# Third graph transposed by vector squares behind the degrees' strips, the last graph's product order, and one pair of activations on VectorE

## The chip, the cores and the metric

One NeuronCore of a Trainium2 chip runs the kernel. The metric is the device time of one execution in microseconds (us); the time before is the median of three runs. TensorE (PE) multiplies matrices and transposes through an identity, VectorE (DVE) does elementwise work and statistics, ScalarE (ACT) activations and copies out of PSUM, GpSimd (POOL) elementwise work on SBUF and some DMA issues, and SyncE (SP) only issues DMAs. Each engine executes its own instructions in program order and waits at semaphores; everything is float32.

## The reference

Two graph layers over x of 16 graphs x 1024 nodes x 256 channels with one adjacency of 1024 x 1024.

```python
# layer 0
h = jnp.maximum(_layernorm(x, axis=-1), 0.0)
fea = jnp.transpose(h, (0, 2, 1)); c_adj = jnp.mean(fea, axis=1)
diff = c_adj[:, None, :] - c_adj[:, :, None]
A = jnp.abs(jnp.abs(jax.nn.sigmoid(diff) - 0.5) - 0.5) * 2.0
Wg = adj[None, :, :] * (A + jnp.transpose(A, (0, 2, 1))) * 0.5
q = relu(einsum('bcn,bnm->bcm', fea, Wg) * para)      # split into 4 heads
k, v = split(h @ kv_w)                                 # 4 heads of 64
x = x + softmax(q k^T * scale) v
# layer 1
h = jnp.maximum(_layernorm(x, axis=-1), 0.0)
A_norm = adj + I
deg = A_norm.sum(0) + A_norm.sum(1) - diagonal(A_norm)
agg = (A_norm * rsqrt(deg)[:, None] * rsqrt(deg)[None, :]) @ h
y1 = relu(batchnorm(agg @ W1.T + b1))                  # over all graphs and nodes
x = x + batchnorm(y1 @ W2.T + b2)
```

The batch norms run over all graphs, so their statistics need every graph's products first.

## The kernel before

**Stages.** `attention()` walks over the 16 graphs. Each graph b has 16 steps (4 units of a channel half and a node half, 4 steps each). A step issues the scores of two key tiles (`scores`, L1081), their exps on ScalarE (L1089), the accumulation of the exps on VectorE (L1110, L1113) and the product with the values of the step before (L1124). Between the steps a generator, `background(b)`, supplies the other work in pieces: the keys, values and queries of graph b+1, the second layer's products of graph b-1, norms. What a generator yields is the cost of its piece; 1.71 stands for one piece of eight or so matmuls. A step takes pieces while `done < due`, where `due = total * (step + 1) / 16`; `total` (L1256 to 1259) is thus the pace, and larger than the sum of the costs when the work shall be done ahead of the stage's end. In the last graph `due` is lowered by a further term. A yield of `TOP` puts the next piece at the head of the following step, between scores and values.

**Weaving.** `weave(main, (start, side), ...)` takes one piece of main and then, from piece `start` on, one slot of each side. Sides are ScalarE, VectorE, GpSimd and DMA work and mostly cost 0. When main has ended, what is left of the sides is run through. `soon(action)` queues an action behind the next piece.

**The stage of graph 0.** `background(0)` (L964) first turns graph 1's normed x (`transposed`, 8 TensorE transposes per channel half through PSUM and ScalarE copies, L424 and L430). Then come the keys and values of graph 1 (`keys_values`, 4 + 4 pieces, L174), its queries (`plain_queries`, 16 pieces) and, at the sides: the weights of graph 1 (`weigh`, 17 slots: Abs L508 and Tanh L516 on ScalarE, a product with adj L495 on VectorE in every other slot), the first norm of graph 2 (`Norm(2, True).all()`, 8 slots), the Strassen combinations of the transposed adjacency (`graph`, GpSimd, 8 chunks), and the degrees (`degrees`). Before, four pieces of keys run with two weight slots each; the four pieces of values come at the end, between the two transposed halves of graph 2.

`degrees` loads eight strips of 128 rows of the transposed adjacency (`load_adj_t`, L226), sums each by an in-place ScalarE copy with an accumulator (L241) and takes the diagonal on VectorE (L243, L244). The strips and the adj tiles of the weights (`load_adj`, L192) have one tag in a pool of three buffers, and both loads are issued by SP. A buffer comes free when the last instruction that uses its tile has run.

**Graphs from 3 on** are turned by `squares` instead: VectorE transposes all 32 x 32 squares of a channel half (L438), the result is stored to DRAM (L442), and `gathered` loads it back in four DMAs that put the squares in place (L452).

**The last graph and the end.** `aggregate(15)` multiplies the normed x with seven blocks of the adjacency (Strassen, L174 `pa`), and its additions (L729 to L758) fill at[0] and at[1], the two node halves; the last block completes the lower half of at[0]. `plain_hidden(15)` then makes eight products (`py`): j, the quarter of the hidden units, is the outer loop, g, the node half, the inner. Each is activated (L910), stored (L911) and goes into the statistics (L914), which are aggregated for a j once both g are in (L916). From the fourth product on each is followed by `next(turns[0])`, one turn of `second()`, the second phase: affine parts of the first batch norm (L96, L97, L1386 to L1388), first activations of graph 0 (`relu`, L1453), and after the last product: `relu(1, 0)`, the differences t1s (L1600), `relu(2, 0)`, `relu(3, 0)`, the affine parts of the other half. Then the first products of the phase are issued in this order: m1 of graph 0, m5 of graph 0 (reads t1s), m1 of graph 1, and `graph(0)` with m2, m3, m6, m7, m4; before m4, `combine_4` on GpSimd (L1486) waits until m6 has read its input.

`normed_last()` is woven into the last hidden products of graph 14: it normalises graph 15's halves as soon as the attention has completed them, so that `aggregate(15)` can begin.

Of the kernel before, what the change touches and what calls it, by code (L numbers as in the profile page):

```python
# [12 lines left out]
ALU = mybir.AluOpType  # L13
# [10 lines left out]
def gnn_two_layers_kernel(  # L24
# [12 lines left out]
    nc = tc.nc  # L37
    B, N, C = x.shape
    H1 = w1_t.shape[1]
    NT = N // P  # L40
    CC = C // P
# [3 lines left out]
    NH = N // FB  # L45
# [28 lines left out]
    hsq_d = [dram.tile([P, CC, N], F32, name=f"hsq_d{b}") for b in range(B)]  # L74
# [24 lines left out]
    def layers(shifted):  # L99
# [51 lines left out]
        def weave(main, *sides):  # L151

            for i, cost in enumerate(main):
                for start, side in sides:
                    if i >= start:
                        cost += next(side, 0.0)
                yield cost
            for _, side in sides:
                yield from side

        def double(slots):

            for _ in slots:
                next(slots, None)
                yield 0.0
# [244 lines left out]
        TOP = -1.0  # L410

        def transposed(b, ks, halves=range(NH), meanwhile=None):

            h = hs["a", b]
            for k in ks:
                if 0 in halves:
                    ht = p3.tile([P, N], F32, tag="ht", name=f"ht_{b}_{k}")
                    hts.setdefault(b, []).append(ht)
            for g in halves:
                pts = [bank(f"htp_{b}_{k}_{g}") for k in ks]  # L420
                for j in range(FB // P):
                    t = g * (FB // P) + j
                    for k, pt in zip(ks, pts):
                        nc.tensor.transpose(  # L424
                            pt[:, j * P : (j + 1) * P], h[:, t, k * P : (k + 1) * P], ident
                        )
                    if meanwhile is not None:
                        meanwhile()
                for k, pt in zip(ks, pts):
                    nc.scalar.copy(hts[b][k][:, g * FB : (g + 1) * FB], pt)  # L430

        def squares(b):

            for k in range(CC):
                sq = p1.tile([P, N], F32, tag="sq", name=f"sq_{b}_{k}")
                nc.vector.transpose(  # L438
                    sq.rearrange("p (i t s) -> p i t s", i=NS, s=SQ),
                    hs["a", b][:, :, k * P : (k + 1) * P].rearrange("p t (i s) -> p i t s", s=SQ),  # L440
                )
                nc.gpsimd.dma_start(out=hsq_d[b][:, k], in_=sq)  # L442
                for _ in range(3):
                    yield 0.0

# [448 lines left out]
        def plain_hidden(b):  # L894

            at = ats[b]
            parts = [(g, j) for g in range(NH) for j in range(HC)]
            if b == B - 1:

                parts.sort(key=lambda part: part[1])  # L900
                next(turns[0])
            for n, (g, j) in enumerate(parts):
                i = b * NH + g
                made = bank(f"py_{i}_{j}")
                for k in range(CC):
                    product(
                        made, later["w1"][:, k, j * P : (j + 1) * P], at[g][:, k, :], k == 0, k == CC - 1
                    )
                y = py.tile([P, FB], F32, tag="y", name=f"y_{i}_{j}")
                nc.scalar.activation(y, made, AF.Identity, bias=b1[:, j : j + 1])  # L910
                nc.gpsimd.dma_start(out=y1_d[i][:, j, :], in_=y)  # L911

                def stats(y=y, i=i, j=j):
                    nc.vector.bn_stats(stats1[:, j, i, :], y)  # L914
                    if i == B * NH - 1:
                        nc.vector.bn_aggr(mv1[:, j, :], stats1[:, j].rearrange("p a s -> p (a s)"))  # L916

                soon(stats)
                if b == B - 1 and n >= len(parts) // 2 - 1:
                    soon(lambda: next(turns[0]))  # L920
                yield 1.71
# [42 lines left out]
        def background(b):  # L964

            if b == 0:
                differences(1)
                for k in range(CC):
                    yield TOP
                    transposed(1, (k,))  # L970
                    yield 1.0
                w, products, norm = weighers[1], keys_values(1), Norm(2, True).all()
                yield from weave(islice(products, 4), (0, double(islice(w, 8))))
                asked, build, sums = plain_queries(1), graph(), degrees()
                yield from weave(
                    islice(asked, 13),
                    (0, w),
                    (4, norm),
                    (5, islice(build, 8)),
                    (7, islice(sums, 6)),  # L980
                )
                differences(2)
                yield from weave(asked, (0, build), (0, sums))
                w = weighers[2]
                yield from islice(products, 1)
                yield from weave(islice(products, 2), (0, islice(w, 2)))
                yield TOP
                transposed(2, (0,))
                yield 1.0
                yield from weave(islice(products, 1), (0, islice(w, 1)))  # L990
                yield from islice(w, 1)
                yield TOP
                transposed(2, (1,))
                yield 1.0
                yield from islice(w, AHEAD - 4)
                yield from products
                return
            before = hidden(b - 1)
            gather = aggregate(b - 1)
            if b + 1 < B:  # L1000
                w, products, norm = weighers[b + 1], keys_values(b + 1), normed(b - 1)
                yield from weave(islice(products, 4), (0, islice(w, 4)))
                asked = queries(b + 1)
                yield from weave(islice(asked, 7), (0, double(w)))
                if b == 1:
                    load_later()
                yield from weave(asked, (2, islice(norm, 5)))
                if b + 2 < B:
                    load_x(b + 2, True)
                yield next(gather)  # L1010
                yield from weave(products, (0, norm))
            else:
                yield next(gather)
                yield from weave(endings.pop(), (2, normed(b - 1)))
            if b + 2 < B:
                yield from weave(gather, (0, summed(b + 2)), (1, lately()))
                yield from prepare(b + 2, before)
            elif b + 2 == B:

                yield from weave(gather, (1, lately()))  # L1020
                endings.append(before)
            else:
                yield from weave(gather, (1, lately()))
                yield from weave(before, (0, normed_last()))
# [215 lines left out]
        def attention():  # L1240
# [6 lines left out]
            bg, done, total, top = iter(()), 0.0, 0.0, False  # L1247
            for s in range(len(steps) + 2):
                if s < len(steps):
                    unit, g = steps[s]  # L1250
                    b = unit.at[0]
                    if s % per_graph == 0:
                        run(bg)
                        top = False
                        bg, done = background(b), 0.0
                        total = (37.6 if b > 0 else 41.0) * (b + 1 < B) + 24.0 * (b > 0) + 6.0 * (b == 0)  # L1256
                        total += 12.0 * (0 < b < B - 2) + 25.7 * (b == B - 1) + 3.0 * (b == 0)

                        total -= 10.3 * (b == B - 1)
                    made = scores(*unit.at, g)  # L1260
                    due = total * (s % per_graph + 1) / per_graph
                    if b == B - 1:
                        due -= 0.5 * min(s % per_graph + 1, (per_graph - 1 - s % per_graph) * 0.75)
                else:
                    due += 5.1
# [46 lines left out]
        with st:  # L1312
            if shifted:
                for b in range(B):
# [13 lines left out]
                    norm = Norm(b, False)  # L1328
# [6 lines left out]
            else:  # L1335
# [7 lines left out]
                norm = Norm(0, True)  # L1343
# [26 lines left out]
    def second(kind):  # L1370
# [54 lines left out]
        with st:  # L1425
# [23 lines left out]
            def relu(i, half, js=range(JH)):  # L1449
                scale, sh = aff[half]  # L1450
                for j in js:
                    y = ys[i][:, half * JH + j, :]
                    nc.scalar.activation(  # L1453
                        y, y, AF.Relu, bias=sh[:, j : j + 1], scale=scale[:, j : j + 1]
                    )
# [137 lines left out]
            yield  # L1593
            relu(0, 0, (1,))
            yield
            relu(1, 0)
            second_steps(0)
            b11, b12, _, _ = inputs(0)
            for j in range(JH):
# [128 lines left out]
```

## Time and profile before

| what | us |
|---|---|
| median of three runs | 2458.16 (2457.94 to 2458.37) |
| profiled execution, its own time | 2458.76 |
| its span, first to last instruction | 2457.0 |
| granted TensorE clock, mean | 0.993 |
| stage of graph 0 (first scores to first scores of graph 1) | 54.6 to 160.1 |
| last scores of the attention | 2123.2 |
| aggregate(15) begins | 2144.1 |
| first product of the second phase | 2184.4 |
| last product of the second phase | about 2380 |

Each trace line names a time in us from the start of the span, a duration, the engine, the line of the kernel, and "out<-in" by the program's names; `x` is how many instructions a line merges. What stands in brackets is the idle time of the engine before it and what ended it. The lines of waits give the total, the number and the longest. The lines of one tile or one source line give the minimum, median and maximum duration in ns. Instructions on TensorE are pipelined, so their durations overlap, and the distance between two starts tells what one costs. Completions of DMAs are read from the semaphore events in the trace.

### The profile page before, as it was taken

What the parts mean: (1) busy time and instruction counts of PE and PEld (TensorE: products, weight loads), DVE (VectorE), ACT (ScalarE), POOL (GpSimd) and SP (SyncE); (2) the same over time, 40 slices, a digit from 0 to 9 for tenths busy, and PEclk for the clock granted to TensorE, in tenths of its full rate; (3) what the DMA queues carried; (4) which work ended last, traced back from release to release, by engine and by line L of the source; (5) the groups of instructions that cost most, each with busy time, mean ns of one, the idle gap of its engine ahead of it and who ended that gap; (6) DMA issues with size and microseconds to landing.
All of it is one profiled execution on the core that took longest, in us unless ns stands there. A gap on an engine that the chain in (4) does not pass through costs nothing. (4 is left out here: it accounts for less than half of the span.)

```text
span 2457.0 us, 35930 instructions
## 1 busy us (share of the span) xinstructions
PE 2411.6 (98%) x13290; PEld 831.1 (34%) x13290; DVE 2006.6 (82%) x3104; ACT 1258.2 (51%) x1870; POOL 555.9 (23%) x644
## 2 busy tenths in 40 slices
PE   9999999999999999999999999999999999999994
PEld 4333333333333333333333333333333332334444
DVE  5688888988888888889898888888888878767775
ACT  7774554545464545545454646454454534345554
POOL 1371202111111212020111112121202103136652
PEclk9999999999999999999999999999999999999997
DMA  4675545363545554453636355544535353456559
GB/s 146 199 247 179 171 137 184 114 233 125 204 143 193 171 189 163 148 177 122 214 120 226 122 200 165 195 158 169 172 130 198 116 201 142 144 206 231 194 193 373
DMA packets 204553, 437.18 MB, mean 178 GB/s; under 512 B 21456, under 2 KB 96720, under 8 KB 200272
## 3 DMA queue, kind: packets, MB, share of 16 engines
q1 hardware_dynamic: 173328, 327.29, 39.7%
q0 software_dynamic: 31040, 107.50, 11.7%
q8 instruction: 107, 1.75, 0.3%
q14 instruction: 78, 0.64, 0.1%
HBM read 331.36 MB, written 103.35 MB: 177 GB/s over the span
## 5 line engine op out<-in xcount | busy, mean ns | idle before, releaser
L1089 ACT ACTIVATE p<-sc 128x1024 f32<-128x1024 f32 x512 | 495.4, 1020 | 649.6 <-PE sc L1081 649.6
L1113 DVE TENSOR_TENSOR acc<-acc,p 128x1024 f32<-128x1024 f32 x384 | 471.1, 1227 | 58.7 <-ACT p L1089 37.3
L1081 PE MATMUL sc<-q,k 64*64 64x512 f32 x4096 | 498.5, 602 | 0.5 <-ACT p L1089 0.5
L1124 PE MATMUL o<-p,v 128*64 128x512 f32 x2048 | 494.6, 604 | 0.0
L174 PE MATMUL pa<-aht,h_b 128*64 128x512 f32 x1536 | 346.0, 592 | 1.1 <-ACT h_b L368 1.1
L174 PE MATMUL pg<-w,x_h 128*64 128x512 f32 x1472 | 332.0, 592 | 0.0
L1081 PEld LDWEIGHTS sc<-q,k 64*64 64x64 f32 x4096 | 131.4, 132 | 336.4 <-issue 287.4
L1124 PEld LDWEIGHTS o<-p,v 128*64 128x64 f32 x2048 | 124.4, 136 | 297.9 <-issue 251.3
L1142 POOL DMA_DIRECT2D out_d<-os x58 | 32.9, 568 | 803.1 <-DVE os L1138 803.1
L495 DVE SCALAR_TENSOR_TENSOR w<-w,adj 128x1024 f32<-128x1024 f32 x128 | 166.0, 1297 | 44.8 <-ACT w L516 44.0
L174 PEld LDWEIGHTS pa<-aht,h_b 128*64 128x64 f32 x1536 | 110.0, 137 | 220.7 <-issue 207.4
L174 PEld LDWEIGHTS pg<-w,x_h 128*64 128x64 f32 x1472 | 105.6, 137 | 210.2 <-issue 198.5
L508 ACT ACTIVATE w<-cbc,csum 128x512 f32<-128x512 f32 x256 | 170.3, 716 | 0.0
L516 ACT ACTIVATE w<-w 128x1024 f32<-128x1024 f32 x128 | 135.6, 1059 | 2.5
L571 DVE TENSOR_TENSOR w<-w,w 128x1024 f32<-128x1024 f32 x112 | 134.4, 1230 | 1.5
L174 PE MATMUL pv<-kvw_f,ht 128*64 128x256 f32 x1024 | 116.1, 379 | 0.0
L174 PE MATMUL pk<-ht,kvw_f 128*64 128x512 f32 x512 | 115.2, 592 | 0.2 <-ACT ht L430 0.2
L174 PE MATMUL py<-at,w 128*64 128x512 f32 x464 | 112.6, 593 | 0.8 <-DVE at L729 0.7
L174 PE MATMUL py<-at,w1s 128*64 128x512 f32 x448 | 107.9, 595 | 0.0
L1453 ACT ACTIVATE yin_f<-yin_f,sm_f 128x512 f32<-128x512 f32 x128 | 93.5, 803 | 25.4 <-DMA yin_f<-y_d 24.4
L826 POOL DMA_DIRECT2D y_d<-y x112 | 61.6, 550 | 145.1 <-DVE y L846 75.7
L1160 DVE TENSOR_REDUCE part<-acc 128x16 f32<-128x512 f32 x128 | 87.8, 686 | 4.4
(198 smaller groups left out, 2962.2 us busy)
## 6 DMA issues: line engine op xcount, KB each, us to landing
aht<-aht_d SPq DMA_DIRECT2D x224, 512.0 KB
adj<-in_adj_dram SPq DMA_DIRECT2D x128, 512.0 KB
y_d<-y POOLq DMA_DIRECT2D x128, 256.0 KB, 3.0
yin_f<-y_d SPq DMA_DIRECT2D x32, 1024.0 KB
para<-in_para_dram SPq DMA_DIRECT2D x64, 256.0 KB
x_d<-x_x POOLq DMA_DIRECT2D x16, 1024.0 KB, 5.1
xo_f<-x_d SPq DMA_DIRECT2D x32, 512.0 KB
out_dram<-xo_f POOLq DMA_DIRECT2D x32, 512.0 KB, 11.1
```

Source lines behind the costliest of these rows:

```text
L174: nc.tensor.matmul(dst[r], left[:, r], right, start=start, stop=stop)
L495: nc.vector.scalar_tensor_tensor(w, w, 1.0, a, op0=ALU.add, op1=ALU.mult)
L508: nc.scalar.activation(w[:, t, :].rearrange("p (t q) -> p t q", q=P), cbc[:, q * NT // NH : (q + 1) * NT // NH], AF.Abs, bias=csum[:, th * ...
L516: nc.scalar.activation(made[i], made[i], AF.Tanh, scale=-0.5 / C)
L571: nc.vector.tensor_sub(block(i)[part], block(x)[part], block(y)[part])
L826: nc.gpsimd.dma_start(out=y1_d[i][:, j, :], in_=y)
L1081: nc.tensor.matmul(sc[part, e, :], ks[b][k][r, m * P + c * HW : m * P + (c + 1) * HW], qs[b][k][r, f * FB : (f + 1) * FB], start=True, sto ...
L1089: nc.scalar.activation(pr, sc, AF.Exp)
L1113: nc.vector.tensor_add(self.acc, self.acc, pr)
L1124: nc.tensor.matmul(self.o[r, :], vs[b][k][:, m, r], pr[:, e, :], start=(m == 0), stop=(m == NT - 1),)
L1160: nc.vector.tensor_reduce(self.part[:, e, :], acc.rearrange("p (c s) -> p c s", s=SQ), AX.X, ALU.add)
L1453: nc.scalar.activation(y, y, AF.Relu, bias=sh[:, j : j + 1], scale=scale[:, j : j + 1])
```

## The change

- `squares(2)` is used for graph 2 as well, with its stores issued by SP instead of GpSimd for this graph; the 16 TensorE transposes, their four copies and their two `TOP` pieces go.
- The stage of graph 0 is put in another order: two weight slots, all eight pieces of keys and values with one weight slot each, then nine pieces of queries with the weights, the norm of graph 2, the combinations and the degrees at their side, all from the first piece or the second; then `differences(2)` and the other seven pieces with the squares, the last chunk and four weight slots of graph 2; then both gathers and two more slots.
- The pace: 2.0 less in the stage of graph 0, 1.7 less in that of the last graph.
- In the last graph's hidden products the node halves swap their order within each j, and the aggregation of the statistics follows.
- The two activations of `relu(1, 0)` become, for each of two blocks, a multiply-add and a maximum on VectorE, in place.

```diff
@@ -439,7 +439,8 @@
                     sq.rearrange("p (i t s) -> p i t s", i=NS, s=SQ),
                     hs["a", b][:, :, k * P : (k + 1) * P].rearrange("p t (i s) -> p i t s", s=SQ),
                 )
-                nc.gpsimd.dma_start(out=hsq_d[b][:, k], in_=sq)
+                queue_of = nc.sync if b == 2 else nc.gpsimd
+                queue_of.dma_start(out=hsq_d[b][:, k], in_=sq)
                 for _ in range(3):
                     yield 0.0
 
@@ -897,7 +898,7 @@
             parts = [(g, j) for g in range(NH) for j in range(HC)]
             if b == B - 1:
 
-                parts.sort(key=lambda part: part[1])
+                parts.sort(key=lambda part: (part[1], -part[0]))
                 next(turns[0])
             for n, (g, j) in enumerate(parts):
                 i = b * NH + g
@@ -912,7 +913,7 @@
 
                 def stats(y=y, i=i, j=j):
                     nc.vector.bn_stats(stats1[:, j, i, :], y)
-                    if i == B * NH - 1:
+                    if i == (B - 1) * NH:
                         nc.vector.bn_aggr(mv1[:, j, :], stats1[:, j].rearrange("p a s -> p (a s)"))
 
                 soon(stats)
@@ -970,30 +971,20 @@
                     transposed(1, (k,))
                     yield 1.0
                 w, products, norm = weighers[1], keys_values(1), Norm(2, True).all()
-                yield from weave(islice(products, 4), (0, double(islice(w, 8))))
+                yield from islice(w, 2)
+                yield from weave(products, (0, islice(w, 8)))
                 asked, build, sums = plain_queries(1), graph(), degrees()
                 yield from weave(
-                    islice(asked, 13),
-                    (0, w),
-                    (4, norm),
-                    (5, islice(build, 8)),
-                    (7, islice(sums, 6)),
+                    islice(asked, 9), (0, w), (0, norm), (1, islice(build, 8)), (0, sums)
                 )
                 differences(2)
-                yield from weave(asked, (0, build), (0, sums))
                 w = weighers[2]
-                yield from islice(products, 1)
-                yield from weave(islice(products, 2), (0, islice(w, 2)))
-                yield TOP
-                transposed(2, (0,))
-                yield 1.0
-                yield from weave(islice(products, 1), (0, islice(w, 1)))
-                yield from islice(w, 1)
-                yield TOP
-                transposed(2, (1,))
-                yield 1.0
+                yield from weave(
+                    asked, (0, squares(2)), (0, build), (3, islice(w, 4))
+                )
+                for k in range(CC):
+                    gathered(2, k)
                 yield from islice(w, AHEAD - 4)
-                yield from products
                 return
             before = hidden(b - 1)
             gather = aggregate(b - 1)
@@ -1254,9 +1245,9 @@
                         top = False
                         bg, done = background(b), 0.0
                         total = (37.6 if b > 0 else 41.0) * (b + 1 < B) + 24.0 * (b > 0) + 6.0 * (b == 0)
-                        total += 12.0 * (0 < b < B - 2) + 25.7 * (b == B - 1) + 3.0 * (b == 0)
-
-                        total -= 10.3 * (b == B - 1)
+                        total += 12.0 * (0 < b < B - 2) + 25.7 * (b == B - 1) + 1.0 * (b == 0)
+
+                        total -= 12.0 * (b == B - 1)
                     made = scores(*unit.at, g)
                     due = total * (s % per_graph + 1) / per_graph
                     if b == B - 1:
@@ -1593,7 +1584,13 @@
             yield
             relu(0, 0, (1,))
             yield
-            relu(1, 0)
+            for j in range(JH):
+                scale, sh = aff[0]
+                y = ys[1][:, j, :]
+                nc.vector.tensor_scalar(
+                    y, y, scale[:, j : j + 1], sh[:, j : j + 1], op0=ALU.mult, op1=ALU.add
+                )
+                nc.vector.tensor_scalar_max(y, y, 0.0)
             second_steps(0)
             b11, b12, _, _ = inputs(0)
             for j in range(JH):
```

## The prediction

> **What bounds the kernel now.** I read the page's busy line first, then what TensorE waited for, then the stretches that the diff touches.
>
> ```profile
> PE 2411.6 (98%) x13290; PEld 831.1 (34%) x13290; DVE 2006.6 (82%) x3104; ACT 1258.2 (51%) x1870; POOL 555.9 (23%) x644
> PE pt_f L1654 <- ACT y_f L1645: 5.8, 2, 5.2
> PE pa L174 <- ACT h_b L368: 1.1, 1, 1.1
> PE m_f L1491 <- POOL t_f L1486: 0.8, 1, 0.8
> PE py L174 <- DVE at L729: 0.7, 1, 0.7
> PE m_f L1491 <- POOL sm_f L96: 0.6, 1, 0.6
> ```
>
> TensorE (PE) is busy 98% and its waits (total, times, longest) are a handful. Its starts are regular: 0.423 us between two product groups, 0.52 at a change between scores and values. I list the gaps above 0.56 us: outside the first 6 us and the last 80 there are nine, 0.65 us beyond the rhythm at 55.9, 1.22 at 2147.1, 0.23 at 2151.8, 0.83 at 2170.2, 0.64 and 0.77 at 2185.0 and 2186.6, 0.21 at 2194.4, 0.93 at 2198.1, 0.13 at 2206.0. So the time moves by what PE no longer issues, by those gaps, and by new ones. The tail behind 2377 is the drain of the outputs and untouched.
>
> **Squares for the third graph.** The stage of the first graph loses 16 TensorE transposes.
>
> ```profile
> L424 PE MATMUL htp<-ident,x_h x32: 272/273/329, 58.9 to 157.9; 128*128 128x128 f32 x32
> L438 DVE STREAM_TRANSPOSE sq<-x_h x26: 1232/1234/1239, 262.9 to 1884.3; 128x1024 f32<-128x1024 f32 x26
> L452 SPq DMA_DIRECT2D ht<-hsq_d x104: 302/430/1088, 267.4 to 1906.2; - x104
> ```
>
> Starts tell more than durations (they overlap): eight transposes hold PE from 150.590 to 151.613, 1.02 us, and as long at 157.1. **Term 1: -2.05 us.** Four copies of 0.59 leave ScalarE. Added: two VectorE transposes of 1.23, two stores (a store of this kind lands in 3.0 to 9.4 us) and eight gathers on SP (0.43 apart, landed 2.6 to 4.9 after issue). Cover: the stage now has 24 pieces and two transposes costing 43.04 in all, paced over 48, so 3.0 a step; it is finished in step 13 of 0 to 15. The second transpose is at piece 20 (step 12), its store lands some 12 us later, the gathers 6 us after that, and the first keys of graph 2 come about 9 us later still. Queued behind the two waiting stores on SP are only the next graph's first adj loads, needed two pieces later. If that cover fails, PE waits for what is late.
> The Trainium skill (VectorE: DVE Perf Modes, Rules for kernel authors) says to transpose 128x128 on TensorE where PSUM will do, which speaks against this: engine for engine 1.02 is cheaper than 1.23, and by it this term would be +0.4. Here PE is full and VectorE is not.
>
> **The degrees' strips move forward.** This edit looks free. I think it is the dear one. Keys and values now all come first; the strips (`degrees`) start at piece 8 instead of 11, when the weights of graph 1 are only at slot 10 of 17 (before: 15). Strips and weights share three "adj" buffers. Before, a strip's load waited for at most one weight:
>
> ```profile
> 92.51 1.22 DVE L495 SCALAR_TENSOR_TENSOR w<-w,adj 128x1024 f32<-128x1024 f32 x1
> 93.75 9.20 SPq L226 DMA_DIRECT2D at<-in_adj_t_dram  x2
> 106.33 1.05 ACT L241 ACTIVATE at<-at 128x1024 f32<-128x1024 f32 x1
> ACT at L241 <- DMA at<-in_adj_t_dram: 2.9, 2, 2.7
> ```
>
> The reader is to see a load issued right behind the VectorE product that frees its buffer, and ScalarE waiting for a strip already now, harmlessly. After the change two adj tiles are still held, so loads run one at a time, each behind a VectorE step, and the row sum on ScalarE that waits for one has the exps queued behind it, which PE needs. Worked from step 5 (87.8, time 0; a step is 3.74 us plus 1.71 a piece; steps 5, 6, 7 have 2, 2, 1 pieces): the product of weight 4 ends at 5.9 as above; strip 0 is issued, lands 3.4 later (its row now) at 9.3; row sum to 10.5; VectorE's diagonal to 11.2, its waiting fold to 12.6, two accumulations (1.23) to 15.1, weight 5 to 16.3. That frees the buffer of strip 2: issued 16.4, landed 3.65 later (the second strip's row) at 20.0, row sum to 21.2. Only then come step 7's exps, the first done at 22.2. PE wants to start step 8 at 19.9. **Term 2: +2.3 us.** The eight strips now land in 3.4 to 6.9 us, mean 5.0. With 5.0, and VectorE stretched beside GpSimd (1.57 for 1.23, 1.4 for 1.22, both in the trace), the same chain ends at 24.7, and with a second stall of 0.7 behind it costs 5.5. Below: a first landing of 3.0 or earlier releases make it nothing. I take 2.3, since the graph's own loads, which crowd the queues at 103 to 124 (DMA share 0.73 to 0.97), start only at piece 9. The rest of the reordering costs nothing: per piece ScalarE has 3 to 4.5 us of work against 3.9 of PE, and a lag of 4.5 us at 80.8 now costs PE nothing.
>
> **Pace of the last graph.** Total 37.7 instead of 39.4, one piece (1.71) less by the end of the attention. With the fillers of 0.1 that `normed` yields, I count one piece left over for the end instead of none. It runs between the last attention output and aggregate(15):
>
> ```profile
> 2144.12 3.60 PE L174 MATMUL pa<-aht,h_b 128*64 128x512 f32 x16
> 2148.78 4.80 PE L174 MATMUL pa<-aht,h_b 128*64 128x512 f32 x20 [1.05 <-ACT h_b L368]
> 2171.41 1.08 PE L174 MATMUL py<-at,w 128*64 128x512 f32 x4 [0.66 <-DVE at L729]
> ```
>
> The first bracket is the wait for the last norm; 1.71 of cover removes 1.22 and the 0.23 behind it. **Term 3: -1.45** (0 if the norm's chain moves along).
>
> **Order of the last products.** The second bracket: the first product wants at[0], whose lower half is finished last (L746, L729 end at 2171.35). With column half 1 first, at[0] is wanted 1.71 after 2169.72, at 2171.43. **Term 4: -0.83**; bound 0.
>
> **Second activations on VectorE.** Two activations (0.72 apart) leave ScalarE; four in-place ops go to VectorE, ahead of the differences that PE's second product m5 waits for.
>
> ```profile
> 2186.06 1.02 DVE L916 BATCH_NORM_AGGREGATE mv<-stats 128x2 f32<-128x192 f32 x1
> 2187.00 1.22 DVE L1600 TENSOR_TENSOR t_f<-yin_f,yin_f 128x512 f32<-128x512 f32 x2
> 2187.77 1.96 PE L1491 MATMUL m_f<-t_f,combined_f 128*128 128x512 f32 x4 [0.60 <-POOL sm_f L96]
> L210 DVE COPY cb_c<-csum 128x512 f32<-128x512 f32 x2 | 0.8, 422 | 2.8 <-ACT h_a L368 2.8
> ```
>
> VectorE is the late one: the differences start as the aggregate ends. No row has a one-tensor scalar op of 128x512; the nearest are the COPY, 0.42, and two-tensor ops, 0.69 (L1600 itself 0.65). I take 0.42, also a one-tensor op: four are 1.7, so m5 starts at 2189.5. Six products (1.72 each) run through; m6 ends at 2198.1, GpSimd's 2.35 (L1486) follows, m4 starts at 2200.5 instead of 2199.46. Part is given back because later gaps close. **Term 5: +1.05**; at 0.69, +2.1; at the 0.15 of the tiniest ops +0.2. A gain I exclude: nothing put before L1600 can bring it forward. ScalarE's freed 1.4 us does not help, since its next halves wait for the affine steps, also on VectorE.
> The Trainium skill (VectorE: DVE Perf Modes, The perf-mode tier table) gives one-tensor fp32 ops in SBUF the double rate and two-tensor ops the single one; its 1227 ns for 2048 elements makes, as an estimate, 0.3 for 512, and the term about +0.6. The same page's rule to keep the count of chained ops down speaks against splitting the activation in two.
>
> **Sum.** -2.05 +2.3 -1.45 -0.83 +1.05 = -0.98. The profiled execution took 2458.76 (span 2457.0, 1.76 around it), so 2457.78; the median 2458.16 stands 0.60 below it: **2457.2**.
>
> **Rivals.**
> A, the strips cost nothing: the buffers come free earlier, or the lag stays inside the 5 us that a step of two pieces allows. For it: today's 2.9 us of such waits cost PE nothing. Against: the chain misses step 8 by 2.3. Time 2457.2 - 2.3 = **2454.9**.
> B, slower than before: the loads land as on average, 5.0. For it: five of eight strips took over 4.6. Against: those were issued in bunches. Time 2457.2 + 3.2 = **2460.4**. From a stall of 3.3 on the whole is a loss; from 8.2 on by over 0.2%, which takes landings of some 6.5 us.
> C, the change doesn't do what it says at the end: the norm's chain moves along with the piece, and VectorE runs at 0.69: +1.45 +1.05, **2459.7**.
>
> **How the numbers follow.** Forecast 0.45 (own range 2455.7 to 2459.0), A 0.20, B 0.20, C 0.10, something unseen 0.05. Best terms together (-4.1) give 2454.0 and the worst (-2.05 +5.5 -0.83 +2.1) 2462.9. Range 2454.0 to 2461.8. Over 0.2% (4.9 us, about what a measurement of this kernel can tell from no change) faster needs a gain that I can't see: 0.10, half from A's edge; slower comes from B's edge and the unseen: 0.13; within 0.77.
>
> **What would show it.** The later profile should have no transposes of graph 2 at 150 to 158, a PE gap of about 2 us near 107 behind a ScalarE wait for a strip's load, no gap at the start of aggregate(15) nor in its first products, and one of 2 to 3 us in front of m5. I am wrong if PE shows no gap near 107 (A), several there (B), or waits for ht before graph 2's keys.

## The result and the profile after

| | before | after |
|---|---|---|
| median of the runs (7 each) | 2458.16 us | 2466.13 us |
| lowest and highest | 2457.94, 2458.84 | 2464.07, 2470.07 |
| profiled execution, its span | 2458.76, 2457.0 | 2464.07, 2462.3 |

After to before is 1.0033 (95% interval 1.0021 to 1.0045): slower by 8 us, outside the forecast's range of 2454.0 to 2461.8. The runs after spread over 6 us, those before over 1; the profiled execution is the fastest of the seven. Lines behind L443 of the kernel before are moved by up to 9.

The busy line of the page after, and TensorE's waits in it (total, times, longest):

```profile
PE 2415.3 (98%) x13274; PEld 833.0 (34%) x13274; DVE 2010.2 (82%) x3110; ACT 1254.8 (51%) x1864; POOL 558.1 (23%) x644
```

```profile
PE sc L1072 <- ACT p L1080: 4.0, 2, 3.5
PE m_f L1482 <- DVE t_f L1597: 2.4, 1, 2.4
...
PE pa L174 <- ACT h_b L368: 0.7, 1, 0.7
```

PE has 16 instructions fewer and is busy 3.7 us longer: some of what is left runs slower. Two waits are new, 3.5 us for exps and 2.4 us for the second phase's differences. The wait for the last norm is 0.7 instead of 1.1, the wait of py for at is gone, and graph 2's keys wait for nothing.

The first place, ScalarE's rows of the timeline (start, duration, and in brackets the idle time before and its releaser):

```profile
103.70 1.06 ACT L241 ACTIVATE at<-at 128x1024 f32<-128x1024 f32 x1 [2.03 <-DMA at<-in_adj_t_dram]
104.67 0.19 ACT L241 ACTIVATION_READ_ACCUMULATOR at<-at 128x1 f32 x1
104.76 1.04 ACT L517 ACTIVATE w<-w 128x1024 f32<-128x1024 f32 x1
108.58 1.06 ACT L241 ACTIVATE at<-at 128x1024 f32<-128x1024 f32 x1 [2.78 <-DMA at<-in_adj_t_dram]
109.55 0.19 ACT L241 ACTIVATION_READ_ACCUMULATOR at<-at 128x1 f32 x1
109.64 1.92 ACT L1080 ACTIVATE p<-sc 128x1024 f32<-128x1024 f32 x2
```

and PE's rows of the same execution:

```profile
101.56 1.95 PE L1072 MATMUL sc<-q,k 64*64 64x512 f32 x16
...
105.32 1.89 PE L174 MATMUL pg<-w,x_h 128*64 128x512 f32 x8
110.70 3.69 PE L1072 MATMUL sc<-q,k 64*64 64x512 f32 x16 [3.49 <-ACT p L1080]
114.32 1.11 PE L1192 MATMUL ot<-ident,os 128*128 128x128 f32 x4
115.36 2.56 PE L1115 MATMUL o<-p,v 128*64 128x512 f32 x8
```

The row sum waits for its strip, step 7's exps stand behind it, and step 8's scores wait for these: the predicted stall at the predicted place. But look at the durations of PE: 3.69 us for sixteen score matmuls that took 1.95 a step earlier. The windows of the same stretch say why (length, then busy time and count of PE, PEld, DVE, ACT, POOL, then the granted TensorE clock, DMA share, GB/s):

```profile
102.00:107.00 5.00, 5.00 (x36) 1.48 (x28) 4.96 (x10) 2.10 (x3) 4.90 (x6) 1.00 0.24 58
107.00:111.00 4.00, 0.51 (x6) 0.30 (x8) 1.82 (x10) 2.42 (x4) 3.90 (x7) 0.85 0.94 310
111.00:114.00 3.00, 3.00 (x16) 0.49 (x8) 2.90 (x3) 2.94 (x7) 2.92 (x3) 0.50 1.02 383
114.00:117.00 3.00, 3.00 (x14) 1.35 (x12) 2.00 (x2) 0.50 (x1) 2.72 (x5) 0.56 0.61 214
117.00:120.00 3.00, 3.00 (x18) 0.98 (x16) 2.25 (x5) 3.00 (x6) 2.98 (x5) 1.00 1.04 359
```

After the idle stretch the clock was granted at half for two of its windows, 6.83 us in the trace's record of the clock. The same behind the gap in front of m5, in windows of the second phase:

```profile
2187.00:2190.00 3.00, 2.27 (x6) 0.59 (x4) 2.97 (x5) 2.82 (x5) 0.79 (x2) 1.00 0.45 175
2190.00:2193.00 3.00, 0.82 (x1) 0.50 (x2) 2.86 (x9) 1.40 (x2) 1.01 (x2) 0.83 0.00 0
2193.00:2196.00 3.00, 3.00 (x6) 1.21 (x5) 1.32 (x2) 2.87 (x5) 0.00 (x0) 0.61 0.00 0
2196.00:2200.00 4.00, 4.00 (x11) 1.85 (x10) 3.14 (x4) 3.17 (x6) 0.00 (x0) 1.00 0.00 0
```

```profile
2192.18 3.54 PE L1482 MATMUL m_f<-t_f,combined_f 128*128 128x512 f32 x4 [2.43 <-DVE t_f L1597]
```

Here it was 3.41 us. Before, the record shows a lower clock only in the drain of the outputs, behind the wait of 5 us at 2380.

The accounts of the two profiled executions, from PE's starts (from here on a gap is the distance between two starts, which without a wait is 0.42 to 0.52 us): strips +6.4 (gap from 0.52 to 4.08, so 3.56; then 7.05 us from step 8's scores to the next product group against 4.23 in a run without the stall, so 2.8), squares -2.05, pace -0.40, order -0.83, second activations +3.02 (from the second matmul of m1 to m4, 17.51 against 14.49). Sum +6.1; the attention began 0.66 earlier for reasons of the start-up, which leaves +5.5, and the spans differ by 5.3.

### The profile page after: what moved, and what is told of

Read it like the earlier page. It is cut to its first block, busy times and chain, and to the rows that moved or that the text cites. A ratio compares the mean times of both kernels' runs of the same rounds, so it can differ in the third digit from the quotient of the medians.

```text
span 2462.3 us, 35903 instructions
## 1 busy us (share of the span) xinstructions
PE 2415.3 (98%) x13274; PEld 833.0 (34%) x13274; DVE 2010.2 (82%) x3110; ACT 1254.8 (51%) x1864; POOL 558.1 (23%) x644
## 3 DMA queue, kind: packets, MB, share of 16 engines
q8 instruction: 107, 1.75, 0.3%
## 5 line engine op out<-in xcount | busy, mean ns | idle before, releaser
L1444 ACT ACTIVATE yin_f<-yin_f,sm_f 128x512 f32<-128x512 f32 x126 | 92.2, 802 | 24.1 <-DMA yin_f<-y_d 22.2
L1101 DVE TENSOR_TENSOR acc<-p,p 128x1024 f32<-128x1024 f32 x64 | 78.6, 1228 | 17.4 <-ACT p L1080 17.4
```

What stands on the lines that cost most here:

```text
L1101: nc.vector.tensor_add(self.acc, self.held, pr)
L1444: nc.scalar.activation(y, y, AF.Relu, bias=sh[:, j : j + 1], scale=scale[:, j : j + 1])
```

## The experiments

All kernels below were timed in turn with the kernel before; ratios are to it, with 95% intervals. Medians of before were 2458.2 to 2458.4.

**1. Strips late.** The strips go to about where they stood before.

```diff
-    islice(asked, 9), (0, w), (0, norm), (1, islice(build, 8)), (0, sums)
+    islice(asked, 9), (0, w), (0, norm), (1, islice(build, 8)), (5, islice(sums, 4))
...
-    asked, (0, squares(2)), (0, build), (3, islice(w, 4))
+    asked, (0, squares(2)), (0, build), (0, sums), (3, islice(w, 4))
```

> The changed kernel with the degrees' strips moved back to about where they stood before: four of them from piece 5 of the first weave on, the rest in the second weave, so that the first row sum on ScalarE stands before step 10's exps instead of step 7's, and no strip shares the three adj buffers with the long run of weights. Theory (a strip that lands late holds ScalarE, the exps queue behind it, TensorE idles 3.5 us near 107, and its granted clock then halves for some 6.8 us, which costs another 2.8): both disappear, -6 to -7 us against the changed kernel in its profiled run, about 2458 to 2459 as median. Rival (the new order of keys, values and norm, or the squares themselves, cost the time): a gap near 107 and the low clock stay, 2464 or more.

Measured 2464.68 (2462.64 to 2467.19), ratio 1.0027 (1.0016 to 1.0037): 1.5 below after, not 7. The gap at 107 and its low clock were gone, as the theory has it. A new gap of 2.72 us stood at 143.4, with 3.41 us at half clock behind it. See the third run, which has the same stage.

**2. Activations back on ScalarE.**

```diff
-            for j in range(JH):
-                nc.vector.tensor_scalar(y, y, scale[:, j : j + 1], sh[:, j : j + 1], ...)
-                nc.vector.tensor_scalar_max(y, y, 0.0)
+            relu(1, 0)
```

> The changed kernel with the second activations of the second phase back on ScalarE. Theory (the four VectorE operations hold the differences back by 1.8 us, the gap in front of m5 becomes 3.0 us, and the clock then halves for 3.4 us): -3.0 us against the changed kernel, 2463 as median, gap in front of m5 1.2 us, granted clock 1.00 through the first products of the second phase. Rival (only the wait counts, no clock): -1.1 to -1.3. Rival (ScalarE's two activations come back and cost their own 1.4): no change.

Measured 2463.92 (2461.81 to 2466.40), ratio 1.0021 (1.0012 to 1.0030): -2.2 in the medians. The gap in front of m5 was 1.19 again, no low clock behind it, and the way from m1's second matmul to m4 took 14.49 as before: the theory's 3.0 in the stage, less in medians that spread over 5 us. In this profile the strips' gap was there with 3.67 us and no low clock behind it, and a second one of 2.91 us at 133.7 brought the half clock instead. So the place at 107 is seen here with the wait and without the slow clock:

```profile
111.04 2.00 PE L1072 MATMUL sc<-q,k 64*64 64x512 f32 x16 [3.08 <-ACT p L1080]
```

The scores take 2.00 us instead of 3.69, and the next product group starts 4.28 us behind them instead of 7.05.

**3. Both.** Edits 1 and 2 together.

> The changed kernel with both undone: strips late and the activations on ScalarE. What stays is the squares, the pace and the order of the last products. Theory: the two costs add, 2454.5 to 2456 (before, less 2.05 for the squares, 0.4 for the pace and 0.83 for the order, less 0.0 to 0.7). Rival (the squares or the new order cost something by themselves): 2457 or more.

Measured 2460.94 (2459.34 to 2462.33), ratio 1.0010 (1.0001 to 1.0019), 5 above the expectation. My undoing had made a stall of its own. SP's rows:

```profile
129.94 1.30 SPq L470 DMA_DIRECT2D csum_d<-csumt  x4
133.10 0.34 SPq L474 DMA_DIRECT2D cbc<-csum_d  x1
133.54 0.38 SPq L443 DMA_DIRECT2D hsq_d<-sq  x1
134.04 2.39 SPq L226 DMA_DIRECT2D at<-in_adj_t_dram  x3
```

and what came of it on ScalarE:

```profile
143.17 1.06 ACT L241 ACTIVATE at<-at 128x1024 f32<-128x1024 f32 x1 [8.82 <-DMA at<-in_adj_t_dram]
```

The last strips now stood on SP behind `differences(2)`, whose load of cbc waits for its stores, and behind a square's store; issued at 134.0, the next one landed 9.0 us later. Whether its place on SP or the traffic made it late was not tried. So runs 1 and 3 show that the place at 107 is free without early strips, and nothing of their price elsewhere.

**4. Needless work in the gaps.** 24 transposes of the identity ahead of step 8's scores, 20 ahead of m5.

```diff
+            pad = ps.tile([P, FB], F32, tag="pz", name=f"pad_{kind}")
+            for i in range(20):
+                nc.tensor.transpose(pad[:, i % NS * P : (i % NS + 1) * P], ident, ident)
             opened["m5"] = product("m5_0", s1, t1s[0])
```

> The changed kernel with idle TensorE transposes of the identity put into the two gaps: 24 ahead of step 8's scores, 20 ahead of m5. The waits stay as they are; TensorE only does needless work in them. Theory (a gap of about 3 us or more halves the clock after it): the clock stays at 1.00 behind both places, step 8's starts are 0.42 to 0.47 us apart instead of 0.83 to 0.99, and the time falls by 3 to 4.5 us, about 2462, although TensorE does more. Rival (the slow starts behind the gaps come from operands that are late, or from a throttle that counts work and not idleness): the starts stay slow and the time is unchanged or 1 us longer.

Measured 2464.46 (2462.43 to 2466.69), ratio 1.0026 (1.0016 to 1.0035). In front of m5 it was as the theory has it; PE's rows, and the windows:

```profile
2190.06 2.35 PE L1612 MATMUL pad_f<-ident 128*128 128x128 f32 x20
2192.65 1.96 PE L1486 MATMUL m_f<-t_f,combined_f 128*128 128x512 f32 x4 [0.25 <-DVE t_f L1601]
```

```profile
2190.00:2193.00 3.00, 2.75 (x22) 2.40 (x21) 2.93 (x7) 1.87 (x3) 1.26 (x2) 1.00 0.13 52
2193.00:2196.00 3.00, 3.00 (x8) 1.33 (x7) 1.73 (x5) 2.39 (x4) 0.00 (x0) 1.00 0.03 5
```

The products wait as long for the differences, but the four matmuls that start with m5 now take 1.96 us instead of 3.54, and the way to m4 is 15.94 instead of 17.51. So 1.57 of the 3.02 us was clock. Nor was the full clock luck of the moment: an estimate from the starts and the clock record is that without the transposes 2.41 us of one clock window of 3.41 would have been idle there, close to the 2.45 that brought the half clock in the kernel after (last section). At 107 the trial failed: the transposes waited 3.36 us themselves, for a PSUM bank that VectorE was late to free, and filled nothing. Instructive all the same: TensorE was idle for 3.5 us there and the clock stayed at 1.00.

**5. Buffers for the strips.** The order of the change stays; the strips lie in the three idle ht buffers.

```diff
-            tile_ = p3.tile([P, N], F32, tag="adj", name=f"{name}_{t}")
+            tile_ = p3.tile([P, N], F32, tag="ht", name=f"{name}_{t}")
```

> The changed kernel in its own order, but the degrees' strips lie in the three buffers of the transposed x (tag ht), which are idle in that stage, instead of sharing the three adj buffers with the weights' loads. Nothing else is moved. Theory (the strip's load waits on SP for a VectorE product to free its buffer, and that is what makes it late): the wait of ScalarE for strips in front of step 8 falls from several us to under 1, the gap near 107 (3.5 us over the rhythm) and the low clock behind it disappear, -4 to -7 us against the changed kernel; the gap in front of m5 stays. About 2460. Rival (the loads are late because the queues are crowded or because the row sums simply come too early for any buffer): the gap stays within 1 us of what it was, 2464 or more.

Measured 2460.63 (2458.39 to 2462.82), ratio 1.0009 (1.0000 to 1.0018): -5.5. ScalarE's waits between 80 and 130, after:

```profile
ACT at L241 <- DMA at<-in_adj_t_dram: 12.0, 5, 4.4
```

and with the strips in their own buffers:

```profile
ACT at L241 <- DMA at<-in_adj_t_dram: 0.2, 1, 0.2
```

12 us of waiting became 0.2, the gap and the low clock at 107 were gone. The strips were late because their loads waited for buffers, which is the prediction's chain; neither the place of the row sums nor the queues' load was the cause. New waits of 1.0 and 0.8 us appeared at 157 and 165.

**6. Half of the activations on VectorE.** On top of 5: one block on ScalarE, one on VectorE.

```diff
-            for j in range(JH):
+            relu(1, 0, (1,))
+            for j in range(1):
```

> As strips_own_buffers, but only the first of the two blocks of the second activations is on VectorE (two operations instead of four), the other back on ScalarE. Theory (the price of the four operations is 1.8 us of wait, and 1.2 to 1.7 more because the wait leaves TensorE idle for about 70% of a 3.4 us clock window): with a gap of 2.0 to 2.1 us the idle share stays under a half, the granted clock stays 1.00 behind m5, and 2 of the 3.0 us come back though only half of the operations went: about 2458.6 against 2460.63. Rival (the price is in proportion to the operations): -1.5, half of 3.0, with slow starts behind m5 still there; or no change, if the block on ScalarE is the later one.

Measured 2459.37 (2457.16 to 2461.03), ratio 1.0005 (0.9996 to 1.0014): -1.26 where 2 was expected. The stage itself, where no noise from the first graph reaches:

```profile
2185.00:2188.00 3.00, 1.91 (x5) 0.98 (x6) 2.88 (x7) 2.76 (x5) 0.81 (x1) 1.00 0.00 0
2188.00:2191.00 3.00, 3.00 (x9) 1.33 (x8) 0.67 (x2) 3.00 (x5) 0.00 (x0) 1.00 0.00 0
```

Gap 2.23, clock 1.00, 15.14 us to m4: half of the operations cost 0.65 of the 3.02 us. The price is not in proportion.

**7. Both dear edits away.** Buffers as in 5, activations on ScalarE.

> As strips_own_buffers, with the second phase's activations back on ScalarE too. What is left of the change: the squares, the order in the first graph's stage, the pace and the order of the last products. Theory: both dear edits are gone, -2.05 - 0.40 - 0.83 against before, 2455 (2454.5 to 2456.5), a kernel faster than both. Rival (the squares' gathers or the new order in the stage of the first graph have a price of their own, as the stall of 0.6 us ahead of graph 2's keys in the run with late strips suggests): 2457 to 2459.

Measured 2458.77 (2455.16 to 2461.56), ratio 1.0001 (0.9992 to 1.0010): the rival. Its fastest runs are where the theory has them, its others are not; in the profile TensorE waits 1.34 us at 157 for VectorE's part and 0.57 and 0.54 at 164 and 166 for ht.

**8. The endings alone.** The kernel before with order and pace.

```diff
-                parts.sort(key=lambda part: part[1])
+                parts.sort(key=lambda part: (part[1], -part[0]))
...
-                    if i == B * NH - 1:
+                    if i == (B - 1) * NH:
...
-                        total -= 10.3 * (b == B - 1)
+                        total -= 12.0 * (b == B - 1)
```

> The kernel before with two edits of the change alone: the order of the last graph's products and the pace of the last graph (12.0 instead of 10.3). Theory: -0.83 for the order (the gap in front of the first py product is gone) and -0.40 for the pace, 2457.2 against 2458.4. Rival (my forecast for the pace, 1.45 of gaps covered): 2456.1. Rival (given back later in the second phase, which waits for the affine steps in any case): 2458.4.

Measured 2457.14 (2456.71 to 2457.91), ratio 0.9995 (0.9986 to 1.0004): -1.14 in the medians, -1.30 between the first attention step and m5's gap. Theory.

**9. The last store behind the norm.** GpSimd's rows after show why the pace brought little:

```profile
2149.23 0.54 POOL L912 DMA_DIRECT2D y_d<-y  x1 [1.23 <-ACT y L911]
2149.80 0.24 POOL L96 TENSOR_SCALAR lnsm_b<-mv_b 128x4 f32<-128x4 f32 x1
2150.12 1.04 POOL L97 TENSOR_TENSOR lnsm_b<-lnsm_b,neg_half 128x4 f32<-128x4 f32 x1
```

The store of the extra piece waits for that piece's activation, and the norm's rsqrt stands behind it. The edit, for graph 14 alone, with which 7 was repeated (a) and 8 (b):

```diff
-                nc.gpsimd.dma_start(out=y1_d[i][:, j, :], in_=y)
+                soon(store)
```

> As own_buffers_relu, and graph 14's stores of y are issued by GpSimd one piece later, so that the last one stands behind the norm's rsqrt and no longer ahead of it. Theory (the extra piece of cover brought 0.40 instead of 1.45, because the rsqrt waits on GpSimd for that piece's activation): the gap at the start of aggregate(15) shrinks from 1.25 to at most 0.6 and the next one closes, -0.8 to -1.05 against own_buffers_relu. Rival (the norm's start on VectorE moves along with the piece): no change.

> The kernel before with order, pace and the store behind the norm: nothing of the first graph's stage and nothing of VectorE's activations. Theory: endings_only (2457.14) less 0.8 to 1.05, 2456.2, gap at the start of aggregate(15) gone; so whatever the versions with squares reach below 2456.2 is what the squares are worth. Rival (the store's gain in store_behind_norm, 2.8 in the medians, came from the stage of the first graph by chance): the same 2456.2; over 2457 if the gap does not close here.

Measured (a) 2455.96 (2454.19 to 2460.28), ratio 0.9992 (0.9983 to 1.0001); (b) 2455.81 (2455.55 to 2456.29), ratio 0.9990 (0.9981 to 0.9999). GpSimd in (a):

```profile
2143.58 0.22 POOL L96 TENSOR_SCALAR lnsm_b<-mv_b 128x4 f32<-128x4 f32 x1 [2.20 <-DVE mv_b L346]
2143.89 1.04 POOL L97 TENSOR_TENSOR lnsm_b<-lnsm_b,neg_half 128x4 f32<-128x4 f32 x1
2144.90 1.17 POOL L913 DMA_DIRECT2D y_d<-y  x2
```

The rsqrt waits for VectorE alone, both gaps at aggregate(15) are closed, and (b) is 1.33 below 8. Theory; of (a)'s -2.8 against 7, what goes beyond this is the first graph's noise, since the edit doesn't touch that stage.

**10. What became of the squares.** (a) and (b) of 9 are equal, though only (a) has 2.05 us less of transposes. Two trials with the gathers put earlier, on top of 9a: the first block's gathers between the squares' stores, and the same with graph 2's adj loads later.

```diff
+            parts = squares(b)
+            for k in range(CC):
+                yield from islice(parts, 3)
+                gathered(b, k)
```

> As store_behind_norm, and on SP the four gathers of the third graph's first channel block stand between the two stores of the squares instead of behind both (and behind three adj loads); the second block's gathers follow three pieces later. Theory (in the three runs with own buffers TensorE waits 1.4 to 2 us for ht ahead of and in graph 2's keys near 163, since the gathers are issued only at 146 to 160; the squares so cost the better part of what their transposes cost): the wait for ht disappears, -1.4 to -2 against store_behind_norm, 2454.3, and the runs lie closer together. Rival (the gathers are late because they wait for the second store or for crowded queues, not for their place): the wait for ht stays over 1 us, 2456.

> As gather_early, with the weights of the third graph taken up at piece 6 of that weave instead of piece 3, so that all eight gathers stand ahead of the third graph's adj loads on SP. Theory (place on SP decides): equal to gather_early or up to 0.7 us below it, 2454.0 to 2454.5, no wait for ht. Rival (weights made later come late for queries): a new gap in the stage of the second graph, 2455 or more.

Measured 2457.74 (2455.26 to 2459.79), ratio 0.9996 (0.9987 to 1.0005), and 2458.64 (2457.32 to 2460.89), ratio 1.0003 (0.9994 to 1.0012): worse, both. The wait for ht was gone, but VectorE waited for graph 2's first adj load, 6.13 us in the first trial and 5.28 in the second. In the second, SP issued this load at 155.5, behind gathers that wait for the second store, and not at 143.7 as in 9a. In the first it was issued as early as in 9a, at 143.6, but landed 11.6 us later instead of 6.5; the first block's gathers had gone out just before it, but what slowed it was not tried. SP and VectorE in gather_early:

```profile
143.59 3.24 SPq L192 DMA_DIRECT2D adj<-in_adj_dram  x3
...
141.29 1.25 DVE L438 STREAM_TRANSPOSE sq<-x_h 128x1024 f32<-128x1024 f32 x1 [1.15 <-DMA hsq_d<-sq]
...
155.17 1.61 DVE L503 SCALAR_TENSOR_TENSOR w<-w,adj 128x1024 f32<-128x1024 f32 x1 [6.13 <-DMA adj<-in_adj_dram]
```

PE got a gap of 3.73 us at 155 and the half clock. VectorE's first row shows something else: there is one sq buffer, and VectorE stands until the first square's store has landed (3.00 us in run 7). So a second buffer (a), and with it the squares one piece apart and all gathers four pieces in (b):

```diff
-                sq = p1.tile([P, N], F32, tag="sq", name=f"sq_{b}_{k}")
+                pool, tag = (p3, "ht") if (b, k) == (2, 1) else (p1, "sq")
+                sq = pool.tile([P, N], F32, tag=tag, name=f"sq_{b}_{k}")
```

> As store_behind_norm, but the second square of the third graph lies in a free ht buffer instead of the one sq buffer, so that its transpose on VectorE needn't wait until the first square's store has landed. Theory (VectorE's stop of 1 to 3 us there is what makes queries, weights and the gathers late): the stop is gone, TensorE's waits of 1 to 2 us at 155 to 165 fall under 0.5, 2454.3 to 2455 and runs closer together. Rival (the gathers' place on SP): the wait for ht stays, 2456.

> As squares_two_buffers, and the second square stands one piece behind the first instead of three, and all eight gathers four pieces behind the first square, ahead of the third adj load of graph 2. Theory (buffer and place together): no wait for ht and none for queries, 2453.8 to 2454.5, which is endings_store less the 2.05 of the transposes. Rival (the squares' traffic crowds the queues in a stage whose DMA share is 0.9, and something always lands late): 2455.5 to 2456.5.

Measured (a) 2456.00 (2453.99 to 2458.83), ratio 0.9991 (0.9982 to 1.0000): the buffer alone leaves the median where it was, and in the profile, one of its slowest runs, ht is awaited for 1.97 us. (b) 2454.45 (2453.75 to 2455.28), ratio 0.9984 (0.9975 to 0.9993). SP's rows in (b):

```profile
135.26 1.13 SPq L444 DMA_DIRECT2D hsq_d<-sq  x2
136.44 2.27 SPq L192 DMA_DIRECT2D adj<-in_adj_dram  x2
142.67 8.20 SPq L466 DMA_DIRECT2D ht<-hsq_d  x8
151.21 14.54 SPq L192 DMA_DIRECT2D adj<-in_adj_dram  x4
```

Both stores go out by 136, SP has issued the last gather by 151 instead of 157 to 160 in runs 7, 9a and (a), PE waits for nothing between 140 and 180. From the first attention step to m5's gap (b) is 1.93 shorter than 9b, 2.05 being what the transposes took. It is 3.8 us below the kernel before, the fastest kernel here, and its runs spread over 1.5 us.

## Why the prediction was wrong

**Term 1, squares (-2.05): right in the profiled execution, with less cover than I gave it.** No transposes, no wait for ht. "Queued behind the two waiting stores on SP are only the next graph's first adj loads" left out two things: the single sq buffer, which makes VectorE wait for the first store, and the gathers, which hold SP too. In ten of the twelve other profiles with squares TensorE waits for something between 140 and 175, the longest wait of each 0.6 to 3.1 us (in two of them strips add to it). Where both were mended, in run 10b, the term came to -1.93; the +0.4 of the count engine for engine was not seen.

**Term 2, strips (+2.3): the step that failed. The chain was right; it was too short, and what an idle stretch costs besides itself was put at nothing.** "Strip 2: issued 16.4, landed 3.65 later at 20.0 ... the first [exp] done at 22.2. PE wants to start step 8 at 19.9." Counted from the attention's first scores (54.57 before, 53.91 after), the issue was predicted at 49.6 and came at 50.9, the exp at 55.4 and at 56.7, PE was to be ready at 53.1 and was at 53.2. The 1.3 us by which the issue was late come from weight 4's product, which ended 0.5 later, from strip 0, which landed in 3.6 and not 3.4, and from weight 5's product, which took 1.75 and not 1.2 and whose end released the third issue on SP, at 104.84:

```profile
93.63 11.54 SPq L226 DMA_DIRECT2D at<-in_adj_t_dram  x3
103.07 1.75 DVE L496 SCALAR_TENSOR_TENSOR w<-w,adj 128x1024 f32<-128x1024 f32 x1
```

That makes 3.56 for 2.3. What was missing altogether is the price of the idle stretch itself: 2.8 us of half clock behind it. Together 6.4, beyond even my slow case of 5.5. Run 5 shows the buffers as the cause; that the clock, not late operands, slows what follows is shown by run 2 at this place, where step 8 stood behind a like wait and ran at the full clock, and by run 4 at the other place.

**Term 3, pace (-1.45): -0.40.** My other end, "0 if the norm's chain moves along", was nearly what happened. I had looked at VectorE and ScalarE, and not at GpSimd's queue, on which the piece's store stands ahead of the rsqrt (run 9).

**Term 4, order (-0.83): right**, the gap at py is gone.

**Term 5, activations (+1.05): +3.02, the same step failed.** The four operations took 0.48, 0.43, 0.54 and 0.43 (I had 0.42; the estimate of 0.3 was too low), the last of them right ahead of the differences:

```profile
2191.00 0.43 DVE L1593 TENSOR_SCALAR yin_f<-yin_f 128x512 f32<-128x512 f32 x1
2191.35 1.29 DVE L1597 TENSOR_TENSOR t_f<-yin_f,yin_f 128x512 f32<-128x512 f32 x2
```

VectorE was late by 1.82 where I had 1.7, and of the 0.7 that later gaps were to give back only 0.4 came. The rest is the clock again: 1.57 by run 4, and run 6 with half of the operations costs 0.65.

With the two terms at what they measured (-2.05 + 6.4 - 0.40 - 0.83 + 3.0) the sum is +6.1. The median's +8.0 goes further since the profiled execution was the fastest: in others the stalls fall elsewhere in the first graph's stage (133.7 and 171 in run 2). How much each place takes in the mean of many executions was not measured. Rival A fell; of C the norm's half nearly came true and VectorE's did not; B, slower than before, had the direction for the wrong reason: it rests on landings of 5.0 us, and strip 2 landed in 3.64, as I had taken it.

## What to carry to other kernels

A new idle stretch of TensorE has two prices here, the wait and the slower clock behind it. Below about 2 us of idleness only the first counted; above, the second came as well wherever more than about 2 us fell into one window of the clock, another 1.57 us (one slow window) to 2.8 us (two). Two stalls of over 3 us that lay across two windows (runs 2 and 4) escaped it. When an edit moves loads forward, follow whose buffers they share and what stands behind each waiting instruction on every queue, the DMA-issuing ones among them. Where DMAs in flight have little slack, the run-to-run spread shows it before the median does.

## What the hardware showed that I had not expected

In all sixteen traces the granted clock changes only on a grid of 3.413 us; the position of the grid differs from execution to execution. From PE's starts and the trace's clock record I worked out how long PE stood still in a window of the grid, the rhythm taken off (outside the first 10 us and the drain of the outputs; the windows with the most idleness):

```
run                      at        idle in window   next window
gather_early             155.0     2.91 (85%)       half
after                    106.4     2.79 (82%)       half, and the one behind it
gather_early_adj_late    157.4     2.65 (78%)       half
relu_on_act              133.3     2.48 (73%)       half
after (m5)              2188.6     2.45 (72%)       half
strips_late (m5)        2188.6     2.45 (72%)       half
strips_own_buffers (m5) 2186.3     2.40 (70%)       half
squares_two_buffers      162.5     2.14 (63%)       half
strips_late              144.0     2.07 (61%)       half
filled_gaps              106.3     2.03 (59%)       full
relu_on_act              109.4     1.66 (49%)       full
late_and_relu            143.6     1.65 (48%)       full
relu_on_act              105.9     1.57 (46%)       full
filled_gaps              109.7     1.51 (44%)       full
half_on_vector (m5)     2184.6     1.47 (43%)       full
```

In these runs some 60% of a window is enough, and it is the share of a single window that counts: in filled_gaps 3.5 us of idleness fell on two windows with 59% and 44%, and the clock stayed full; in strips_late a wait of 2.7 us lay so that it brought the half clock. The line between 59% and 61% rests on two runs; by the matmuls' modelled ends instead of their starts it lies between 54% and 58%.

The way back to the full clock asks for more. In `after` PE stood idle for 0.87 us (26%) of the first slow window too, and a second slow one followed. By the modelled ends, with the drain of the outputs counted and the first 10 us left out, every slow window in the sixteen traces that was idle for 19% or more was followed by another, and every one with 12% or less by the full clock. So a stall that reaches far enough into the slow window is paid for twice.

The Trainium skill (TensorE: Matmul & The Clock Gate, Why this matters for your kernels) asks for no idle gaps of TensorE over about 3 us, and its Part 1 has a free-running window of 3413 ns of which one idle one brings the half clock. The durations here, 3.41 and 6.83 us, agree; the limit does not: windows idle for 2.1 to 2.9 us of 3.4 were enough.
